# The end of a router on Trainium2: layer 1's modulation in steps between the slot table's groups, one-hot columns in pairs, a fixed TensorE order, and the last router tiles by twos

## The chip, the cores and the metric

The kernel runs on one core of one Trainium2 chip. The metric is the device time of the whole program in microseconds (us), and it is compared by the median of several runs. TensorE multiplies matrices into PSUM, VectorE (DVE), ScalarE (ACT) and GpSimd (POOL) work beside it, and SyncE (SP) issues most of the DMAs. The program is recorded by a tile framework: each engine has its own queue, which it runs in order, and a scheduler decides the order in the queues at build time, unless the source fixes it.

## The reference

Two transformer layers over 2048 tokens of width 512, in fp32. Each layer takes six modulation vectors from a matrix product of its own conditioning vector; they are needed for the normalisation (scale and shift) and for the gates of that layer's attention and feed-forward part.

```python
mod = (_silu(L1_c) @ L1_wmod).reshape(L1_c.shape[0], 6, 1, -1)
sa, ca, ga, sb, cb, gb = (mod[:, 0], mod[:, 1], mod[:, 2], mod[:, 3], mod[:, 4], mod[:, 5])
```

The feed-forward part of layer 0 is a mixture of 64 experts. A router picks eight experts for each token; experts that are only second choices may be mapped to similar first choices; every token then goes through its experts:

```python
logits = x @ gate_weight.T
probs = jax.nn.softmax(logits.astype(jnp.float32), axis=-1).astype(logits.dtype)
top_val, top_idx = lax.top_k(probs, TOP_K)
...
mapping = jnp.where(replace, best_primary, jnp.arange(E))
rerouted = mapping[top_idx]
...
gu = lax.ragged_dot(xs, jnp.swapaxes(gate_up_proj, 1, 2), group_sizes)
gate, up = jnp.split(gu, 2, axis=-1)
hact = jax.nn.silu(gate) * up
y = lax.ragged_dot(hact, jnp.swapaxes(down_proj, 1, 2), group_sizes)
...
out = jnp.zeros_like(x).at[tok].add(y * w[:, None])
```

Layer 1 has windowed attention and a dense feed-forward part; it needs the modulation of layer 1, and it comes after the experts.

## The kernel before

The kernel goes through layer 0's attention, the router, the experts in 32 pairs, layer 1's attention and layer 1's feed-forward part. The 2048 tokens are 16 tiles of 128. All matrix products go through one helper, `mm` at L129, so the profile names nearly all of them L129; they are told apart by the tiles that they write and read. An fp32 product shows as two instructions in the trace, an f16 product or a transpose as one.

**Router, first part.** It runs inside the attention's loop. After each fourth tile (`m % 4 == 3`), `route` (L417) puts two steps on a list, `logits` (L421) for the next turn of the loop and `choose` (L432) for the one after. `logits` normalises four tiles, transposes them (tiles nT_f, hTr), stores the normalised rows to `h_d` in DRAM, and multiplies by the gate (lg). `choose` takes the softmax and the eight largest values of each token, and leaves `sel` (f16 masks), its transpose `selT` (through st) and the normalised probabilities `pT` (through spT). The attention's own end for tile m is `project` (L383): transposes oT_a, a copy by ACT to oTs_a, and the product po_a, which DVE adds to `x_sb`.

**Router, second part** (from about L531). `cnt` counts the tokens of each expert and DVE copies it to c (L536). Then follow the mapping of experts, the running counts `pf` by token, and `perm`, the order of the experts by size (L599). `gps` gives the weights' row of each expert, and SP starts to load the first four experts' weights. `pw` (L614 to L622) carries the probabilities into the new order and to `h_d`; `ops_` (L637) gives the spill-over offsets that `shift` needs. From `pf` and `shift` DVE makes `vT` (L656 to L659): for each token and expert the slot that the token gets. `tv` transposes it, ACT copies it to `vm`, and `V.max` takes eight slots for each token.

**The slot table.** `tps` is a table in PSUM of 128 rows by 164 columns that ends up with the token of each slot. The 16 tiles go in four groups of four. For each tile DVE writes two one-hot tensors in f16, `hr` (128 rows by 8 choices, L677) and `hc` (164 columns by 8 choices, L680); ACT scales `hr` by the token's number (L678); and eight products add one choice each:

```python
for k in range(TOPK):
    mm(tps, hr[:, :, k], hc[:, :, k], n == 0, n == NT * TOPK - 1)
```

Both operands are read at a step of eight f16. `hr` and `hc` have three buffers each. DVE then turns the table into `tidx` (L687), and POOL gathers rows of `h_d` by it into `xring` (L507), 128 rows at a time and twelve places in all. Two small products, eps_ and rps, make lists for the loop that catches spill-over; DVE makes `of` (L697) between them.

**Modulation of layer 1.** `modulate(1, ...)` (L704) is recorded behind all this. For each of the six vectors a weight tile `wm` of 1 MB is loaded by SP (two buffers). Four vectors are needed as columns; each takes 16 products of 128 x 128 by a single column, 32 instructions in the trace. Two are needed as rows; each takes four products of 128 x 512. Where the scheduler puts these products among those of `tps` is its own choice.

**The first experts.** `turn(0)` transposes the gathered rows of experts 0 and 1 (xp, L734) and writes xT by DVE and ACT; `take(turn(0), 2 * KC)` does all eight of these steps before `gate_up` (L743) starts on the first pair. `shares(0)` copies the gathered probabilities (wc, L883). `fetch_w` and `fetch_x` fetch weights and rows two pairs ahead. `in_turn` (L714) is a scope in which the scheduler records an instruction behind the last TensorE instruction noted in `st_["pe"]`; it fixes an order in the queue and adds no wait on the chip.

Of the kernel before, what the change touches and what calls it, by code (L numbers as in the profile page):

```python
# [17 lines left out]
ALU = mybir.AluOpType  # L18
# [38 lines left out]
NX = 12  # L57

# [65 lines left out]
def block_kernel(ctx: ExitStack, tc: tile.TileContext, t: dict, out: bass.AP):  # L124
# [141 lines left out]
    with tc.tile_pool(name="a0", bufs=1) as ap, tc.tile_pool(name="a0k", bufs=1) as kp:  # L266
# [71 lines left out]
        with tc.tile_pool(name="rn", bufs=4) as rn, tc.tile_pool(name="a0s", bufs=2) as sp, tc.tile_pool(name="p_s", bufs=2, space=PSUM) as p_s, tc.tile_pool(  # L338
# [78 lines left out]
            def route(m, a):  # L417

                g = m - 3

                def logits():  # L421
                    hT = rn.tile([P, KC, D], F32, tag="hT", name=f"hTr_{g}", bufs=1)
                    normed_T(list(range(g, g + 4)), hT, 0, m0[4], m0[3], rn, p_m, "f0", "m", h_d)
                    lg = p_m.tile([P, 4, E], F32, tag="m", name=f"lg_{g}")
                    for b in range(4):
                        for c in range(KC):
                            mm(lg[:, b, :], hT[:, c, b * P : (b + 1) * P], gw[:, c, :], c == 0, c == KC - 1)
                    mx = small.tile([P, 4], F32, tag="lmx", name=f"lmx_{g}")
                    V.tensor_reduce(mx, lg, X, ALU.max)
                    V.tensor_tensor(pb[:, g : g + 4, :], lg, bc(mx, 2, E), ALU.subtract)  # L430

                def choose():  # L432
                    p4 = pb[:, g : g + 4, :]
                    S.activation(p4, p4, AF.Exp)
                    sm = small.tile([P, 4], F32, tag="lsm", name=f"lsm_{g}")
# [6 lines left out]
                    for b in range(4):  # L442
                        i = g + b
                        V.max(top[:, i, :], pb[:, i, :])
                        V.tensor_copy(t4[:, b, 0:4], top[:, i, 0:4])
                        V.match_replace(left[:, 0, b, :], t4[:, b, :], pb[:, i, :], -1.0)
                        V.match_replace(left[:, 1, b, :], top[:, i, :], pb[:, i, :], -1.0)
                    for c in range(2):
                        V.tensor_scalar(sel[:, g : g + 4, c, :], left[:, c], 0.0, None, ALU.is_lt)
                    st = p_m.tile([P, D], F32, tag="m", name=f"st_{g}")  # L450
                    for b in range(4):
                        mm(st[0:E, b * P : (b + 1) * P], sel[:, g + b, 1, :], ident16)
                    S.copy(selT[:, g * P : (g + 4) * P], st[0:E, :])

                    t4s = small.tile([P, 4], F32, tag="t4s", name=f"t4s_{g}")
                    V.tensor_reduce(t4s, top[:, g : g + 4, :], X, ALU.add)
                    V.tensor_scalar(t4s, t4s, 1e-12, None, ALU.max)
                    V.reciprocal(t4s, t4s)
                    V.tensor_tensor(p4, p4, sel[:, g : g + 4, 1, :], ALU.mult)
                    V.tensor_tensor(p4, p4, bc(t4s, 2, E), ALU.mult)  # L460
                    st = p_m.tile([P, 2, P], F32, tag="m", name=f"spT_{g}")
                    for b in range(2):
                        i = g + 2 * b
                        TE.transpose(st[:, b, :], pb[:, i : i + 2, :].rearrange("p i e -> p (i e)"), ident)
                    S.copy(pT[:, g // 2 : g // 2 + 2, :], st)
# [5 lines left out]
            for a in range(len(units) + 4):  # L471
                if a < len(units):
                    soft0(*units[a])
                if 0 < a <= len(units):
                    m, hf = units[a - 1]
                    value0(m, hf)
                    if hf == 1:
                        project(m, heads.pop(m), wo, sp, p_m, "a0")
                        if m % 4 == 3:
                            route(m, a)  # L480
# [24 lines left out]

    def gather(dst, src, idx):
# [18 lines left out]
    with tc.tile_pool(name="rw", bufs=1) as rw, tc.tile_pool(name="rh", bufs=3) as rh:  # L525
        with tc.tile_pool(name="p_q", bufs=3, space=PSUM) as p_q, tc.tile_pool(
            name="p_b", bufs=1, space=PSUM
        ) as p_b:
            id2, own = con("id2"), con("own")
# [71 lines left out]
            mm(gps, con("expert")[0:E, :], perm[0:E, :])  # L601
# [3 lines left out]

            mps = p_q.tile([E, P], F32, tag="q", name="mps")
            TE.transpose(mps, map2, ident)
            mapT = rw.tile([E, P], F32, tag="mapT", name="mapT")
            S.copy(mapT, mps)
            mps = p_q.tile([P, E], F32, tag="q", name="mrs")  # L610
            mm(mps, mapT, perm[0:E, :])
            mapr = rw.tile([P, E], F32, tag="mapr", name="mapr")
            S.copy(mapr, mps)
            pw = rw.tile([P, NT, E], F32, tag="pw", name="pw")  # L614
            pws = [p_q.tile([P, 8, E], F32, tag="q", name=f"pw_{b}") for b in range(2)]
            for a in range(NT // 2):
                for b in range(2):
                    r = slice(E * b, E * b + E)
                    mm(pws[b][:, a, :], pT[r, a, :], mapr[r, :])
            for b in range(2):  # L620
                S.copy(pw[:, b:NT:2, :], pws[b])
            nc.sync.dma_start(out=h_d[0:T, D:].rearrange("(i p) e -> p i e", p=P), in_=pw)  # L622
# [13 lines left out]
            V.tensor_copy(ot, ov_i)  # L636
            ops_ = p_q.tile([P, 2], F32, tag="q", name="ops_")  # L637
            mm(ops_[:, 0:1], con("upto")[0:E, :], ot[0:E, :])
            mm(ops_[:, 1:2], ones[0:E, :], ot[0:E, :])
# [6 lines left out]
            V.tensor_scalar(base1, base, 1.0, None, ALU.add)  # L646

# [4 lines left out]
            tps = p_b.tile([P, ST], F32, tag="tps", name="tps")  # L652
            n = 0
            for b in range(2):
                jump = rh.tile([P, D], F32, tag="jump", name=f"jump_{b}", bufs=2)
                V.tensor_scalar(jump, pf[:, b, :], room, shift, ALU.is_ge, ALU.mult)  # L656
                vT = rh.tile([P, D], F32, tag="vT", name=f"vT_{b}", bufs=2)
                V.scalar_tensor_tensor(vT, pf[:, b, :], base1, jump, ALU.add, ALU.add)
                V.scalar_tensor_tensor(vT, mT[:, b, :], 1.0, vT, ALU.min, ALU.mult)  # L659
                tv = p_q.tile([P, 4, 2, E], F32, tag="q", name=f"tv_{b}")  # L660
                for i in range(4):
                    TE.transpose(tv[:, i].rearrange("p h e -> p (h e)"), vT[:, i * P : (i + 1) * P], ident)
                for h in range(2):
                    i0 = 8 * h + 4 * b
                    i4 = slice(i0, i0 + 4)
                    S.copy(vm[:, i4, :], tv[:, :, h, :])
# [8 lines left out]
                    for i in range(i0, i0 + 4):  # L675
# [3 lines left out]
                        hc = rh.tile([P, ST, TOPK], F16, tag="hc", name=f"hc_{i}")  # L679
                        V.tensor_tensor(hc, iota8[:, 0:ST, :], bc(tlf[:, i, :], 1, ST), ALU.is_equal)  # L680
                        for k in range(TOPK):
                            mm(tps, hr[:, :, k], hc[:, :, k], n == 0, n == NT * TOPK - 1)
                            n += 1

# [19 lines left out]
            m1 = modulate(1, want, modp, rw, p_q, "q")  # L704
# [5 lines left out]
    with tc.tile_pool(name="h1", bufs=1) as h1, tc.tile_pool(name="p_x", bufs=2, space=PSUM) as p_x, tc.tile_pool(  # L710
        name="p_g", bufs=3, space=PSUM
    ) as p_g, tc.tile_pool(name="p_y", bufs=3, space=PSUM) as p_y:

        def in_turn():  # L714

            return tc.issue_after(st_["pe"].ins) if "pe" in st_ else nullcontext()
# [10 lines left out]
        def x_T(r, xs, n):  # L727
# [3 lines left out]
            def chunk(c):  # L731
# [6 lines left out]
                else:  # L738
                    V.tensor_scalar(xT[:, c, 0:n], xp[:, 0:n], sc, sh, ALU.mult, ALU.add)  # L739
# [3 lines left out]
        def gate_up(r, ws, xTs, n, between=None):  # L743

            hA = []
            for h, (w1, xT) in enumerate(zip(ws, xTs)):
                ps = []
# [145 lines left out]
        take(turn(0), 2 * KC)  # L893
        shares(0)
        for r in range(2, 4):
            fetch_x(r)
        for q in range(NQ):
# [3 lines left out]
            if q + 2 < NQ:  # L901
                for r in (2 * q + 4, 2 * q + 5):
                    fetch_w(r)
                    fetch_x(r)
            steps = turn(q + 1) if q + 1 < NQ else []
            with in_turn():
                hA, hB, last = gate_up(
                    q, [s["w"][0] for s in two], [s["xT"] for s in two], ROOM[q], lambda: take(steps, 2)
                )
            take(steps, 2)  # L910
# [334 lines left out]
def _layouts(a):  # L1245
# [10 lines left out]
    for n in (0, 1):  # L1256
        d[f"L{n}_c"] = cols(a[f"L{n}_c"].reshape(D))
        d[f"L{n}_wmod"] = a[f"L{n}_wmod"].reshape(KC, P, 6, D).transpose(2, 1, 0, 3)
# [48 lines left out]
```

## Time and profile before

| what | us |
|---|---|
| median of 3 runs (lowest, highest) | 2306.02 (2305.62, 2310.59) |
| the profiled execution | 2301.6 |
| its span, first to last instruction | 2299.8 |
| TensorE busy | 2122.3 (92%) |
| DVE, ACT, POOL busy | 847.7, 473.6, 559.0 |
| mean granted TensorE clock | 0.941 of full speed |
| last attention projection of layer 0 ends | 310.27 |
| first product of the slot table | 357.55 |
| slot table complete | 412.06 |
| first transpose of gathered rows | 435.94 |
| first product of expert 0 | 441.55 |

The page's section 2 cuts the span in 40 slices of 57.5 us and shows in tenths how busy each engine was and which share of the full clock TensorE was granted. The chain of waits follows the work that ended last back to the start: each row has its start, its length, its engine, the tile it writes, and its line. The windows give busy time by engine (instructions in brackets), the granted clock, the DMA engines' share and GB/s for a stretch of time. In the groups by shape, the number behind the bar is the total busy time in us and the mean of one instruction in ns; neighbours in a queue overlap, so that the distance from start to start can be shorter than the mean.

### The profile page before, as it was taken

Reading aid. Unit: us, or ns where it says so; the run is one execution under the profiler, and the core shown is the slowest. Engines: PE = TensorE matmul, PEld = TensorE weight load, DVE = VectorE, ACT = ScalarE, POOL = GpSimd, SP = SyncE. Lnnn points to the kernel's source line nnn. Section 1 sums busy time; section 2 is a strip of 40 time slices with the busy share of each in tenths; the row PEclk is TensorE's granted clock in tenths of the full one; section 3 lists DMA queues with packets and bytes.
Section 4 is the critical chain, followed back from the end, with each engine's and each line's share of the span. In section 5 each row is a group of like instructions: output and inputs, shape, how many; then the busy total and the mean of one; then the engine's idle time right before and its main releaser. Section 6 shows DMA issues by size and latency. Waiting matters only on the chain.

```text
span 2299.8 us, 27707 instructions
## 1 busy us (share of the span) xinstructions
PE 2122.3 (92%) x10584; PEld 1178.8 (51%) x10584; DVE 847.7 (37%) x2177; ACT 473.6 (21%) x1114; POOL 559.0 (24%) x444
## 2 busy tenths in 40 slices
PE   3999978999999999999639999997999999999999
PEld 3665645545555566676315555554444444444444
DVE  3246655154544433345366456554011011000101
ACT  0124413111111111111001356653010010010000
POOL 2300000365665666654424100000010010010000
PEclk9899975799999999999869899998999999999999
DMA  9800113589899899999752000005000000000000
GB/s 355 299 2 19 38 58 110 166 200 224 220 236 235 208 244 239 253 301 313 163 195 59 19 2 1 2 2 218 2 0 19 0 0 4 15 0 0 19 0 19
DMA packets 137350, 256.40 MB, mean 111 GB/s; under 512 B 52649, under 2 KB 55657, under 8 KB 134657
## 3 DMA queue, kind: packets, MB, share of 16 engines
q1 hardware_dynamic: 95136, 159.48, 20.9%
q0 software_dynamic: 36032, 77.30, 16.2%
q10 hardware_dynamic: 6048, 17.83, 2.1%
q8 instruction: 85, 1.39, 0.2%
q14 instruction: 49, 0.39, 0.1%
HBM read 180.56 MB, written 71.65 MB: 110 GB/s over the span
## 4 chain that ended last, share of the span: by engine, by line
PE 81%; DVE 6%; DMA 6%; ACT 4%; issue 1%; POOL 1%; ACTq 0%; POOLq 0%; SPq 0%; DVEq 0%
PE y L129 18%; PE gu L129 10%; PE up L129 9%; PE gate L129 9%; PE gub L129 5%; PE xp L734 3%; PE q L129 3%; ACT pr L1106 3%; PE s L129 3%; PE po L129 2%; PE mod L129 2%; PE po_a L129 2%; DMA sum<-yo,tidx 2%; PE o L129 2%; PE pt L1124 2%; PE tps L129 2%
## 5 line engine op out<-in xcount | busy, mean ns | idle before, releaser
L793 POOL DMA_INDIRECT sum<-yo,tidx x164 | 268.7, 1638 | 120.6 <-DMA sum<-yo,tidx 36.5
L507 POOL DMA_INDIRECT xring<-h_d,tidx x164 | 168.0, 1025 | 510.9 <-DVE tidx L687 331.3
L1231 DVE SCALAR_TENSOR_TENSOR act<-up,L_ws_up,sg 128x512 f32<-128x512 f32 x64 | 48.1, 751 | 598.6 <-PE up L129 598.6
L129 PE MATMUL gu<-xT,w 128*128 128x312 f32 (+26 forms) x1024 | 245.5, 398 | 6.6 <-DVE xT L739 6.6
L129 PE MATMUL gate<-xh,wug 128*128 128x512 f32 x512 | 230.7, 592 | 0.0
L129 PE MATMUL up<-xh,wug 128*128 128x512 f32 x512 | 230.7, 592 | 0.0
L129 PE MATMUL y<-wd,act 128*128 128x512 f32 x512 | 229.5, 592 | 0.0
L129 PEld LDWEIGHTS gu<-xT,w 128*128 128x128 f32 x1024 | 191.7, 192 | 60.7 <-issue 16.5
L1229 ACT ACTIVATE sg<-gate,L_ws_gate 128x512 f32<-128x512 f32 x64 | 44.0, 687 | 575.4 <-PE gate L129 575.4
L129 PEld LDWEIGHTS up<-xh,wug 128*128 128x128 f32 x512 | 97.3, 190 | 122.5 <-issue 122.5
L129 PEld LDWEIGHTS y<-wd,act 128*128 128x128 f32 x512 | 97.3, 190 | 122.5 <-issue 122.5
L129 PEld LDWEIGHTS gate<-xh,wug 128*128 128x128 f32 x512 | 96.8, 190 | 119.6 <-issue 119.6
L129 PE MATMUL y<-w,hA 128*128 128x512 f32 (+22 forms) x328 | 148.8, 596 | 0.9 <-DVE yo L789 0.9
L789 DVE SCALAR_TENSOR_TENSOR yo<-y,wc,modr 128x512 f32<-128x512 f32 (+22 forms) x164 | 117.1, 745 | 80.1 <-PE y L129 68.4
L737 ACT ACTIVATE xT<-xp,modc,modc 128x312 f32<-128x312 f32 (+26 forms) x128 | 74.3, 580 | 316.0 <-PE xp L734 286.3
L1200 POOL TENSOR_TENSOR xh<-hT 128x1024 f32<-128x1024 f32 x3 | 7.6, 2524 | 503.3 <-DVE xn_f L229 335.9
L1106 ACT ACTIVATE pr<-ng,nb 128x208 f32<-128x208 f32 (+1 forms) x256 | 115.4, 453 | 55.1 <-DVE nb L1096 55.1
L129 PE MATMUL gub<-xT,w 128*64 128x312 f32 (+26 forms) x1024 | 125.4, 398 | 0.0
L734 PEld LDWEIGHTS xp<-cst,xring 128*128 128x128 f32 x656 | 72.3, 141 | 68.1 <-issue 46.6
L734 PE MATMUL xp<-cst,xring 128*128 128x128 f32 x656 | 98.3, 282 | 1.9 <-DVE xT L739 1.2
L755 DVE TENSOR_TENSOR hA<-hA,gu 128x312 f32<-128x312 f32 (+26 forms) x64 | 28.2, 440 | 186.7 <-PE xp L734 99.6
L129 PEld LDWEIGHTS gub<-xT,w 128*64 128x64 f32 x1024 | 70.5, 137 | 44.8 <-issue 11.3
(311 smaller groups left out, 2662.6 us busy)
## 6 DMA issues: line engine op xcount, KB each, us to landing
w<-in_L_gu SPq DMA_DIRECT2D x64, 768.0 KB, 7.3
sum<-xring SPq DMA_DIRECT2D x5, 4352.0 KB, 21.9
w<-in_L_dn SPq DMA_DIRECT2D x64, 256.0 KB, 8.3
wm<-in_L_wmod SPq DMA_DIRECT2D x9, 1024.0 KB, 6.8
w<-in_L_dn SPq DMA_DIRECT2D x64, 128.0 KB, 8.7
sa<-sum SPq DMA_DIRECT2D x32, 256.0 KB, 9.0
h_d<-xn_f SPq DMA_DIRECT2D x16, 256.0 KB, 2.9
wda<-in_L_Wdown SPq DMA_DIRECT2D x8, 512.0 KB, 13.9
```

Source lines behind the costliest of these rows:

```text
L129: return TE.matmul(o, lhsT, rhs, start=start, stop=stop)
L507: return G.indirect_dma_start(out=dst, out_offset=None, in_=src[:, :], in_offset=bass.IndirectOffsetOnAxis(ap=idx, axis=0))
L734: st_["pe"] = TE.transpose(xp[:, b * P : (b + 1) * P], xg[:, c * P : (c + 1) * P], ident)
L737: S.activation(xT[:, c, 0:n], xp[:, 0:n], AF.Identity, bias=sh, scale=sc)
L755: V.tensor_tensor(o[:, 0:n], o[:, 0:n], ps[1][:, 0:n], ALU.mult)
L789: V.scalar_tensor_tensor(yo, ys[h], shares[h][rows, b : b + 1], m0[5][rows, :], ALU.mult, ALU.mult)
L793: G.indirect_dma_start(out=sums[k][:, :], out_offset=bass.IndirectOffsetOnAxis(ap=idx, axis=0), in_=yo, in_offset=None, compute_op=ALU.add,)
L1106: S.activation(prs[i, j][:, c, :nk], ng[:, :nk], AF.Exp, bias=nb, scale=-1.0, accum_out=totals[i][:, c, j : j + 1],)
L1124: TE.transpose(pt[0:n, c, :], pr[:, c, b * P : b * P + n], ident)
L1200: eng.tensor_tensor(b[:, :, 0, :], a[:, :, 0, :], a[:, :, 1, :], ALU.add)
L1229: S.activation(sg, pg, AF.Silu, scale=wsg[:, f : f + 1])
L1231: V.scalar_tensor_tensor(acts[f], pu, wsu[:, f : f + 1], sg, ALU.mult, ALU.mult)
```

## The change

- `route(g, n, a)` takes a number of tiles. The router runs after tiles 4, 8 and 12 with four tiles, and after 14 and 16 with two.
- `in_turn` moves up, and `next_mm` and `next_T` record a product or a transpose behind the last noted one. From `gps` on, the TensorE order is the order in which the source names the instructions. `ops_` stands in front of `pw`, and both `vT` are made before `tv`.
- `hc` becomes four blocks of 164 columns by two choices. `iota8` is read two choices wide, and a product reads `hc` at a step of two f16.
- Layer 1's modulation no longer goes vector by vector but in four steps over the contraction: step k takes one 128-row slice of all six vectors. The weights' layout in DRAM is changed to match. The four column vectors are made as rows on four column groups of the array (32 rows of the result each), then turned by four transposes; the two gates are made with 128 rows. A step stands behind each of the first three groups of the table and one behind the table. `wm` now has one buffer, `wg` two; the load of step k+1 is recorded behind step k.
- The rows of expert 1 are transposed between the two halves of the first `gate_up`, and weights and rows of the third pair are fetched behind it. The wc copies stand behind the last xT that DVE wrote.
- In TensorE's queue, `rps` now stands behind the second group of the table; it stood behind the third.

```diff
+ROUTED = {4: 4, 8: 4, 12: 4, 14: 2, 16: 2}
...
-                        if m % 4 == 3:
-                            route(m, a)
+                        if m + 1 in ROUTED:
+                            n = ROUTED[m + 1]
+                            route(m + 1 - n, n, a)
...
+    def in_turn():
+
+        return tc.issue_after(st_["pe"].ins) if "pe" in st_ else nullcontext()
+
+    def next_mm(*a):
+        with in_turn():
+            st_["pe"] = mm(*a)
...
+            def mod_load(k):
+                w = rw.tile([P, 4, D], F32, tag="wm", name=f"wm_1_{k}")
+                nc.sync.dma_start(out=w, in_=t["L1_wmod"][k, :, 0:4, :])
+                wg = rw.tile([P, 2, D], F32, tag="wg", name=f"wg_1_{k}", bufs=2)
+                nc.sync.dma_start(out=wg, in_=t["L1_wmod"][k, :, 4:6, :])
+                mod_w[k] = w, wg
+
+            mod_load(0)
...
-            mm(gps, con("expert")[0:E, :], perm[0:E, :])
+            next_mm(gps, con("expert")[0:E, :], perm[0:E, :])
...
-            mm(ops_[:, 0:1], con("upto")[0:E, :], ot[0:E, :])
-            mm(ops_[:, 1:2], ones[0:E, :], ot[0:E, :])
+            next_mm(ops_[:, 0:1], con("upto")[0:E, :], ot[0:E, :])
+            next_mm(ops_[:, 1:2], ones[0:E, :], ot[0:E, :])
...
+            mods = [p_b.tile([P, 2, D], F32, tag=g, name=f"mod_{g}") for g in ("mT", "pf")]
+            cs1 = csil[:, 1, :]
+            csb = rw.tile([P, KC, P], F32, tag="csb", name="csb_1")
+            S.copy(csb, bc(cs1, 2, P))
+
+            def mod_step(k):
+                w, wg = mod_w.pop(k)
+                for u in range(4):
+                    next_mm(mods[0][32 * u : 32 * u + 32, 0, :], csb[:, k, 0:32], w[:, u, :], k == 0, k == KC - 1)
+                for u in range(2):
+                    next_mm(mods[1][:, u, :], csb[:, k, :], wg[:, u, :], k == 0, k == KC - 1)
+                if k + 1 < KC:
+                    mod_load(k + 1)
...
-                        hc = rh.tile([P, ST, TOPK], F16, tag="hc", name=f"hc_{i}")
-                        V.tensor_tensor(hc, iota8[:, 0:ST, :], bc(tlf[:, i, :], 1, ST), ALU.is_equal)
+
+                        hc = rh.tile([P, 4, ST, 2], F16, tag="hc", name=f"hc_{i}")
+                        two = tlf[:, i, :].rearrange("p (a c) -> p a c", c=2)
+                        V.tensor_tensor(hc, bc(iota8[:, 0:ST, 0:2], 1, 4), bc(two, 2, ST), ALU.is_equal)
                         for k in range(TOPK):
-                            mm(tps, hr[:, :, k], hc[:, :, k], n == 0, n == NT * TOPK - 1)
+                            next_mm(tps, hr[:, :, k], hc[:, k // 2, :, k % 2], n == 0, n == NT * TOPK - 1)
                             n += 1
+                    if 2 * b + h < 3:
+                        mod_step(2 * b + h)
...
-            m1 = modulate(1, want, modp, rw, p_q, "q")
+            mod_step(3)
+            m1 = {}
+            mrow = rw.tile([P, D], F32, tag="mrow", name="mrow")
+            S.copy(mrow, mods[0][:, 0, :])
+            for u, n in enumerate((2, 5)):
+                m1[n] = modp.tile([P, D], F32, tag=f"mod1{n}", name=f"modr_1_{n}")
+                S.copy(m1[n], mods[1][:, u, :])
+            mcol = mods[0][:, 1, :].rearrange("p (c q) -> p c q", c=KC)
+            for c in range(KC):
+                next_T(mcol[:, c, :], mrow[:, c * P : (c + 1) * P], ident)
...
-        take(turn(0), 2 * KC)
-        shares(0)
+        opening = turn(0)
+        take(opening, KC)
+        with tc.issue_after(st_["xv"].ins):
+            shares(0)
...
                 hA, hB, last = gate_up(
-                    q, [s["w"][0] for s in two], [s["xT"] for s in two], ROOM[q], lambda: take(steps, 2)
+                    q, [s["w"][0] for s in two], [s["xT"] for s in two], ROOM[q], lambda: take(steps, 2),
+                    lambda: take(opening, KC),
                 )
+            if q == 0:
+                fetch(2)
```

## The prediction

> **What bounds the kernel now.** I read the page first (sections 1 and 2), then the chain of waits between 295 and 455 us, where nearly all of the edits lie, then the windows, the groups by shape and the timelines of each engine there.
>
> ```profile
> PE 2122.3 (92%) x10584; PEld 1178.8 (51%) x10584; DVE 847.7 (37%) x2177; ACT 473.6 (21%) x1114; POOL 559.0 (24%) x444
> PEclk9899975799999999999869899998999999999999
> ```
>
> TensorE is the bound nearly everywhere, and its granted clock sags in slices 6 to 8 (287 to 460 us): that is the end of the router. The chain there (start, length):
>
> ```profile
> 347.25 0.76 PE ops__2719 L129 x4
> ...
> 357.55 28.65 PE tps L129 x96
> 386.20 0.93 PE rps L129 x2
> 387.13 13.74 PE mod L129 x64
> 400.87 7.14 PE tps L129 x24
> 408.01 1.71 PE mod L129 x2
> 409.73 2.34 PE tps L129 x8
> 412.06 8.62 PE mod L129 x38
> ...
> 420.70 9.03 DMA wm<-in_L_wmod
> ...
> 429.86 5.41 PE mod L129 x8
> ```
>
> Two things stand out. The 128 matmuls of the slot table take 298 ns each (28.65/96), and layer 1's modulation sits half between them (15.4 us) and half behind them: expert 0's first transposes come only at 435.94 us, 23.9 us after the table. Clock, and what the form of an operand costs:
>
> ```profile
> 312.00:315.00 3.00, 1.79 (x8) 0.98 (x8) 2.10 (x6) 0.26 (x1) 0.00 (x0) 0.81 0.37 134
> 357.00:387.00 30.00, 29.45 (x98) 14.38 (x98) 21.61 (x53) 15.24 (x14) 0.00 (x0) 0.50 0.14 38
> 414.00:417.00 3.00, 3.00 (x9) 1.31 (x7) 0.00 (x0) 0.17 (x1) 2.39 (x3) 0.62 1.03 251
> L680 DVE TENSOR_TENSOR hc<-iota,tlf 128x1312 f16<-128x1312 f16 x16 | 13.4, 834 | 0.0
> L129 PE MATMUL tps<-hc,hr 128*128 128x164 f16 x128 | 38.5, 477 | 2.3 <-ACT hr L678 2.3
> 336.25 0.31 PE L129 MATMUL pf<-ones,acc 128*64 128x128 f16 x1
> 336.36 0.31 PE L129 MATMUL pf<-ltri,selm 128*64 128x128 f16 x1
> 1372.86 1.08 PE L129 MATMUL o<-pts,v 80*32 80x256 f32 x8
> 417.77 0.92 POOL L507 DMA_INDIRECT xring<-h_d,tidx  x1 [0.30 <-issue]
> ```
>
> The column before the DMA share is the granted clock. The pf matmuls, whose moving operand is contiguous, follow each other every 107 ns for 128 columns at the same half clock: 0.83 ns a column. tps takes 1.82 ns a column, with hc read at a step of 8 f16 (16 bytes). The reading is what is slow, not the array.
>
> **The change part by part** (minus is time saved on the path)
>
> *A. The last four tiles of the router by twos.* The path runs from the end of tile 13's output projection po_a (298.69) to the count copy c (331.52): 32.8 us. Afterwards TensorE's fixed order is: lg of 12 and 13, only then oT and po of tile 14, st of 12/13, spT, oT and po of tile 15, then lg of 14 and 15. So the first pair's chain is put in front of the last two projections, and ACT loads Sqrt and Exp tables twice (1.28 us each, from the timeline of ACT). Rows: x_sb add 0.7, bn 0.7, xn 0.56 each, halved hTr about 0.55, lg 1.76 at full clock (32 took 3.52) or 3.55 at half (7.10), choose for two tiles about 3.2 (5.2 for four, 324.98 to 330.2). Laid out: lg of 12/13 ends at 306.9, po of 14 at 311.7, st at 312.4, pb's last multiply at 314.3 (behind a 0.7 add and a 0.7 bn on DVE), oT and po of 15 until 319.4, its add, statistics, xn, transposes until 324.9, lg until 326.6, choose until 329.8, c at 330.8: -0.7. That is with the full clock. In the trace the clock fell to half in the windows that follow one 2.9 us gap of TensorE. Here there are gaps of 2 to 3 us before po of 15 and after it. po takes 3.7 at full, at most 6.8 at half; two of them, transposes and lg all at half give +9. I take +3: po of 15 partly at half (+1.5), the last lg at half (+1.8), transposes (+0.5), less the 0.7.
>
> [...] the window says 0.50 for more than 50 us. The measurement decides: a matmul that waits on its operand does not warm the clock here, while six dense 512-column fp32 matmuls did (0.62, then 0.95 after 417).
>
> *B. ops_ in front of pw.* ot is ready at 343.1, but ops_ stood behind 3.68 us of pw in TensorE's queue and ran at 347.25. Ahead of it, it ends at 344.1; more_f, shift and the two vT follow (348.03 to 351.75 before), so vT of b=0 is ready at 347.8. pw (until 347.8) hides under that DVE work; tv starts at 347.9 in place of 351.88: -3.9. The pw store on SP waits for ACT until 349, earlier than before.
>
> *C. hc as four blocks of pairs.* The bytes are the same, 1312 f16 on DVE, 0.76 us start to start (0.83 mean). But iota8 is now read in pairs at a 16-byte step. No DVE row of the trace does this. [...] By the row alone (0.76) the table would end about 3 us earlier than I sum below. The trace's nearest row is TensorE's own 16-byte step (1.82 ns an element)[...]. I take 1.3, ends 0.76 and 1.75. On the path once at the start: +0.5.
>
> *D. The table.* On TensorE, hc is then read at 4 bytes. By pf's 0.83 ns a column, 164 columns are 137 ns; the weights hr keep their step of 16 bytes, and their load is 145 ns (PEld rows of hr, 142/145/309). I take 145 ns, so a tile of eight is 1.16 us in place of 2.39. DVE needs hr 0.61 + hc 1.3 + 0.23 (tidy-up per tile) = 2.14 us a tile, ACT 1.16: DVE becomes the limit while only tiles run. Between the groups stand three steps of modulation: 4 products of 32 rows on four column groups and 2 of 128. The o row: 8 of 256 columns on column groups, the next such row 0.85 us later (1373.71), half the serial price (po_a: 0.45 for 512). So the four cost 1.7 and the two 1.7 at full clock, 6.8 in all at half; [...] I take 4.7 (between 3.4 and 6.8). hr and hc have three buffers, so DVE runs three tiles ahead during a step. From the first tile: group 1 ends at 5.7, step 0 at 10.4, group 2 at 15.0. Then comes a wait that was not there: rps now stands behind group 2 in TensorE's queue and needs "of", which DVE makes only after hr and hc of the third tile of group 3, and that hr needs group 2's buffers. Hence of at 20.2; TensorE idles 5 us with step 1 and group 3 queued behind. rps to 21.1, step 1 to 25.8, group 3 to 30.5, step 2 to 35.2, group 4 to 39.9. Before: 412.06 - 357.55 = 54.5. So -14.6; -18 with hc at 0.76, -8 with hc at 1.75 and slow steps.
>
> Loads: wm has one buffer now; the next 1 MB leaves SP's queue when four products are done, and lands 5 to 9 us later (6.8 median on the page, 12.2 at most). Steps are 15, 10 and 9 us apart from there, so they just fit.
>
> *E. Behind the table.* Before: 23.9 us to the first xp, 29.5 to the first gu (441.55). After: hole and tidx 0.8, POOL starts at +1.7, its fourth gather at +5.7 (413.76 to 417.77), landing 2.8 to 5.9 us later (the tile view of xring: 2.8 least, 5.9 median). So xp of expert 0 has its rows at +10.3. Meanwhile step 3, mrow 0.6 and four transposes 1.1 end at about +7, hidden under the gathers with 3 us to spare; the ACT copies of the two gates as well. gu of expert 0 begins at +12.7. The other expert's xp (2.9 us, half of the 5.6 that both took) now stands between the two gu[...]. gu of both ended at 453.4, 41.3 after the table; now 12.7 + 5.9 + 1.7 + 2.9 + 5.9 = 29.1: -12 (ends -14 and -8). The wc copies moved behind xT wait for the eighth gather, at +17, with hA at +19 behind them: free. Weights and gathers of experts 4 and 5 are ordered behind gate_up(0), but POOL's order is the same as before and w1 waits for those buffers anyway: nothing, and q=2 needs them 60 us later.
>
> **Sum.** +3 - 3.9 + 0.5 - 14.6 - 12 = -27.0. The profiled execution took 2301.6 us (span 2299.8), so 2274.6; the median of the runs shown is 4.4 above that, 2306.0, and against it I predict 2279.
>
> **The rivals**
>
> 1. The pairs do not shorten tps: the weights' 16-byte step, untouched, sets the 298 ns. For it: PEld of hr and the matmul alternate. Against it: its load takes 145 of the 298. The table would be 38.2 + three steps of 4.7 to 6.8 + 3.4 of rps and its wait, about 58.5: +4 in place of -14.6, in all -8.4, 2298.
>
> 2. The half clock at the end of the router (+9) together with modulation loads that arrive at the 12.2 us maximum (+5.5 before step 2, +2.5 in the tail): -27 + 6 + 8 = -13, 2293. For it: the 0.50 from 315 on. Against it: the wm loads meet fewer gathers than before.
>
> 3. Slower than before, by one mechanism: DVE does not keep its packed rate in L680's new form, with runs of only two elements[...] It decides from about 3.1 us per hc; below that the other gains carry it. [...]
>
> **How the numbers follow.** A measurement of this kernel tells about 0.2% (4.6 us) from no change. Forecast 0.71, rival 1 0.12, rival 2 0.12, rival 3 0.05. Faster: 0.71 + 0.12 + most of rival 1 (0.09) = 0.92; same 0.03; slower 0.05. Best ends together (-0.7, -3.9, 0, -18, -14) are -36.6: 2269; the forecast's worst (+9, -3.9, +1, -8, -8) is about -10. The range 2267 to 2297 holds the forecast, rival 2 and half of rival 1.
>
> **What would show it.** Right: tps starts every 140 to 150 ns within a tile, hc at 1.2 to 1.7 us, an idle TensorE of some 5 us before rps, table under 43 us, the first xp 9 to 12 us after tidx, gu directly behind. A is right if c comes 0 to 6 us later in that part, with the half clock already before po of tile 15. Wrong: tps at 298 ns; hc above 3 us; step 1 or 2 waiting for wm; or a first xp that waits for step 3 and not for its rows.

## The result, and the profile after

| | before | changed kernel |
|---|---|---|
| median, us (lowest, highest; runs) | 2305.82 (2301.39, 2310.59; 4) | 2281.01 (2278.45, 2284.87; 4) |
| ratio, 95% interval | | 0.9893 [0.9869, 0.9918] |
| profiled execution, its span, us | 2301.6, 2299.8 | 2280.16, 2278.2 |
| slot table, first tps to last | 54.5 (357.55 to 412.06) | 36.3 (354.07 to 390.39) |
| last tps to first gub of expert 0 | 41.9 | 34.9 |
| first gub to the end of the span | 1845.9 | 1852.9 |

gu and gub are the products of `gate_up`: gu the first 128 columns of gate and of up, one expert after the other, gub the last 64 columns of both experts.

The change is worth 24.8 us by the medians; 27 were predicted (2306 to 2279). Two further sets of the changed kernel (y1_same and z1_same below) gave ratios of 0.9903 [0.9880, 0.9926] and 0.9882 [0.9860, 0.9905]; the median of all twelve of its runs is 2281.9.

The page after, TensorE's busy time and its granted clock in 40 slices. The sag of slices 6 to 8 is now 0.8 and 0.7 in slices 6 and 7:

```profile
PE 2081.9 (91%) x10492; PEld 1149.6 (50%) x10492; DVE 856.8 (38%) x2193; ACT 477.9 (21%) x1123; POOL 558.6 (25%) x444
PEclk9899987999999999999779899998999999999999
```

TensorE's timeline around the table (start, length, what it did, and in brackets its idle time before and what ended it):

```profile
354.07 2.41 PE L131 MATMUL tps<-hc,hr 128*128 128x164 f16 x16 [2.73 <-ACT hr L725]
...
359.20 1.06 PE L131 MATMUL mod_mT<-wm,csb 128*32 128x512 f32 x8
360.20 1.98 PE L131 MATMUL mod_pf<-wg,csb 128*128 128x512 f32 x4
...
366.80 0.79 PE L131 MATMUL tps<-hc,hr 128*128 128x164 f16 x8 [1.05 <-DVE hc L729]
373.90 0.97 PE L131 MATMUL rps<-of,ones 64*128 64x191 f32 x2 [6.31 <-DVE t8b L717]
374.80 1.94 PE L131 MATMUL mod_mT<-wm,csb 128*32 128x512 f32 x8
376.66 2.73 PE L131 MATMUL mod_pf<-wg,csb 128*128 128x512 f32 x4
379.23 2.02 PE L131 MATMUL tps<-hc,hr 128*128 128x164 f16 x24
```

Eight tps take 0.8 us where they took 2.4, and nearly every tile now waits for DVE's hc or ACT's hr. The new wait stands before rps: 6.31 us. A step takes 3 us at full clock and 4.6 when it starts at half. The windows (us, busy time with instructions of PE, PEld, DVE, ACT, POOL, then granted clock, DMA share, GB/s) show TensorE empty while DVE is full, and after that the full clock:

```profile
354.00:357.00 3.00, 2.77 (x19) 2.52 (x20) 3.00 (x4) 2.21 (x3) 0.00 (x0) 0.50 1.07 317
370.00:373.00 3.00, 0.00 (x0) 0.00 (x0) 3.00 (x4) 2.81 (x3) 0.00 (x0) 0.50 0.00 0
384.00:390.00 6.00, 4.25 (x34) 3.04 (x35) 5.54 (x6) 3.45 (x3) 0.00 (x0) 1.00 0.53 175
```

The groups by shape: hc has become dearer, and tps, in time on the array, 38.5 to 13.5 us.

```profile
L729 DVE TENSOR_TENSOR hc<-iota,tlf 128x1312 f16<-128x1312 f16 x16 | 21.5, 1342 | 0.0
L131 PE MATMUL tps<-hc,hr 128*128 128x164 f16 x128 | 13.5, 259 | 8.3 <-DVE hc L729 5.1 <-ACT hr L725 3.2
```

Behind the table, TensorE's timeline shows the transposes of expert 0's rows starting as the rows land, then expert 0's gu, and a wait inside the transposes of expert 1:

```profile
397.11 0.41 PE L796 MATMUL xp<-cst,xring 128*128 128x128 f32 x2 [3.37 <-DMA xring<-h_d,tidx]
...
399.30 1.12 PE L796 MATMUL xp<-cst,xring 128*128 128x128 f32 x4 [0.97 <-DMA xring<-h_d,tidx]
...
402.80 7.42 PE L131 MATMUL gu<-xT,w 128*128 128x440 f32 x16
...
416.25 1.97 PE L796 MATMUL xp<-cst,xring 128*128 128x128 f32 x8 [5.16 <-DVE xT L801]
```

The chain of waits has a row there whose cause the profile does not name:

```profile
404.67 10.28 another core or an unknown queue x2
414.95 0.60 DVE hA L819
415.55 0.66 DVE xT L801
416.25 1.97 PE xp L796 x8
418.22 6.44 PE gu L131 x16
```

So at the first gub the kernel is 28.7 us ahead of the one before (425.25 against 453.95), and at the end of the span 21.6.

### The profile page after: what moved, and what is told of

Read it like the earlier page. It is cut to its first block, busy times and chain, and to the rows that moved or that the text cites. A ratio compares the mean times of both kernels' runs of the same rounds, so it can differ in the third digit from the quotient of the medians.

```text
span 2278.2 us, 27545 instructions
## 1 busy us (share of the span) xinstructions
PE 2081.9 (91%) x10492; PEld 1149.6 (50%) x10492; DVE 856.8 (38%) x2193; ACT 477.9 (21%) x1123; POOL 558.6 (25%) x444
## 4 chain that ended last, share of the span: by engine, by line
PE 78%; DVE 7%; DMA 6%; ACT 4%; issue 2%; POOL 1%; another core or an unknown queue 0%; ACTq 0%; POOLq 0%; SPq 0%; DVEq 0%
PE y L131 18%; PE gu L131 10%; PE up L131 9%; PE gate L131 9%; PE gub L131 5%; PE xp L796 3%; PE q L131 3%; ACT pr L1179 3%; DMA sum<-yo,tidx 3%; PE s L131 3%; PE po L131 2%; PE o L131 2%; PE po_a L131 2%; PE pt L1197 2%; PE v L131 1%
## 5 line engine op out<-in xcount | busy, mean ns | idle before, releaser
L857 POOL DMA_INDIRECT sum<-yo,tidx x164 | 269.2, 1642 | 119.5 <-issue 37.5
L796 PE MATMUL xp<-cst,xring 128*128 128x128 f32 x656 | 101.0, 286 | 10.5 <-DVE xT L801 5.2
```

Of the source, the lines that this page charges most:

```text
L796: st_["pe"] = TE.transpose(xp[:, b * P : (b + 1) * P], xg[:, c * P : (c + 1) * P], ident)
L857: G.indirect_dma_start(out=sums[k][:, :], out_offset=bass.IndirectOffsetOnAxis(ap=idx, axis=0), in_=yo, in_offset=None, compute_op=ALU.add,)
```

## The experiments

Three questions: what of the table's gain comes from which part; whether the last tiles by twos and the split of the first experts' rows help; and what the row of 10.28 us is. All but the runs on the kernel before start from the changed kernel. "After the table" below is the time from the last tps.

**x1_rps_late.** The wait before rps is taken away.

```diff
-            mm(rps, ones[0:E, :], of)
-            V.tensor_copy(rank_more, rps)
-
             mod_step(3)
+            next_mm(rps, ones[0:E, :], of)
+            V.tensor_copy(rank_more, rps)
```

> The changed kernel, with rps (and rank_more) moved in TensorE's queue from behind the table's second group to behind the last modulation step. Theory: the 6.3 us in which TensorE idles before rps hold up step 1 and the third group, and DVE then stands 4.9 us for a buffer of hr; without the wait the table is as long as DVE's own work, 16 tiles of about 2.1 us: 36.3 us becomes 31 to 32, the whole program 4 to 5 us shorter (2276). Rival: the weights of step 1 have only just landed by then, so TensorE waits for wm in place of rps, and the table stays at 35 us or more.

Measured: 2270.88 (2268.76 to 2272.09), ratio 0.9834 [0.9818, 0.9851]; table 30.8 us. TensorE's timeline at the place of the old wait:

```profile
372.37 0.78 PE L131 MATMUL tps<-hc,hr 128*128 128x164 f16 x8 [1.06 <-DVE hc L729]
373.07 1.06 PE L131 MATMUL mod_mT<-wm,csb 128*32 128x512 f32 x8
374.07 1.98 PE L131 MATMUL mod_pf<-wg,csb 128*128 128x512 f32 x4
376.56 0.84 PE L131 MATMUL tps<-hc,hr 128*128 128x164 f16 x8 [0.51 <-ACT hr L725]
```

Step 1 follows at once; wm was there, so the rival falls. The wait cost the table 5.5 us. The total fell by more than the 4 to 5 us expected, by 11 us against the twelve runs of the changed kernel: gub, too, begins 4.3 us earlier after the table (+30.6 for +34.9), which is taken up with the late semaphores below. No run of the changed kernel is on record from the chip of x1 to x4, so how much of these 4.3 us is the edit's and how much the chip's is not shown.

**x2_contig.** hc's comparison reads adjacent pairs.

```diff
+    iota2 = rp.tile([P, ST, 2], F16, tag="iota2", name="iota2")
...
+            V.tensor_copy(iota2, bc(iota[:, 0:ST], 2, 2))
...
-                        V.tensor_tensor(hc, bc(iota8[:, 0:ST, 0:2], 1, 4), bc(two, 2, ST), ALU.is_equal)
+                        V.tensor_tensor(hc, bc(iota2, 1, 4), bc(two, 2, ST), ALU.is_equal)
```

> The changed kernel, with the pairs that hc is compared to read from a tile of their own in which the pairs are adjacent (164 x 2 f16), in place of iota8 at a step of 16 bytes. Theory: hc went from 0.76 to 1.28 us only because of that step; adjacent pairs bring it back to about 0.76, a tile costs DVE 1.6 us, the table takes about 28 us in place of 36.3, and the program is 8 us shorter (2273) unless the modulation's loads become late. Rival: runs of two elements are what costs DVE (the other operand also changes every two), then hc stays at 1.2 to 1.3 us and the time at 2281.

Measured: 2268.7 (2263.37 to 2275.26), 0.9838 [0.9821, 0.9854]; table 31.5 us. The group by shape:

```profile
L731 DVE TENSOR_TENSOR hc<-iota,tlf 128x1312 f16<-128x1312 f16 x16 | 13.3, 833 | 0.0
```

1342 ns are 833 again, the 834 of the kernel before: the 16-byte step was the whole surcharge, and runs of two elements cost DVE nothing. The table fell by 4.8 us and not by the 8 expected: the wait before rps stayed (4.42 us here) and step 1 behind it ran at half clock (5.4 us).

**x3_before_pairs.** Only the pairs, in the kernel before (the three lines of hc and the product's index from the diff above).

> The kernel before, with hc in four blocks of pairs and nothing else changed. Theory: tps drops from 298 to 150 ns or less each, DVE becomes the limit of the table at 2.1 us a tile, and the table, with the 15.4 us of modulation still in it, takes 43 to 47 us in place of 54.5; program 2306 becomes 2296 to 2298. Rival 1 of the prediction (the weights' step of 16 bytes sets the 298 ns): tps stays at 298 ns and the table at 54 us or more, 2306.

Measured: 2292.13 (2287.62 to 2294.47), 0.9933 [0.9916, 0.9950]; table 40.1 us. The group by shape:

```profile
L129 PE MATMUL tps<-hc,hr 128*128 128x164 f16 x128 | 17.8, 316 | 11.0 <-ACT hr L678 8.7 <-DVE hc L681 1.9
```

The pairs alone take 14.4 us off the table, more than the 7.5 to 11.5 expected, and 15.0 off the first gub (438.93); the time, too, is below the 2296 to 2298 expected. Rival 1 of the prediction falls here. The 12.4 us of modulation inside the table do not cost their full length: behind them the 24 tps of three tiles follow at once, in 3.29 us (392.43), which DVE had made ready meanwhile.

**x4_combo.** x1 and x2 together.

> The changed kernel with both edits: adjacent pairs for hc, and rps behind the last modulation step. Theory: DVE needs about 1.6 us a tile, 25 us in all, and the four steps 3 us each; the table takes 24 to 28 us in place of 36.3, limited by the loads of wm (one buffer, a step at most every 7 us or so): 2269 to 2272. Rival: the loads take 9 to 12 us each, the steps wait, the table stays above 31 us and the gain is no larger than that of one edit alone.

Measured: 2265.58 (2263.86 to 2274.36), 0.9812 [0.9796, 0.9828]; table 27.1 us, 9.3 less than the changed kernel's. A new wait of 1.80 us for wm before step 1 keeps it from the full 5.5 + 4.8.

**y4_eight.** hc back in its old form, all other parts kept.

```diff
-                        hc = rh.tile([P, 4, ST, 2], F16, tag="hc", name=f"hc_{i}")
-                        two = tlf[:, i, :].rearrange("p (a c) -> p a c", c=2)
-                        V.tensor_tensor(hc, bc(iota8[:, 0:ST, 0:2], 1, 4), bc(two, 2, ST), ALU.is_equal)
+                        hc = rh.tile([P, ST, TOPK], F16, tag="hc", name=f"hc_{i}")
+                        V.tensor_tensor(hc, iota8[:, 0:ST, :], bc(tlf[:, i, :], 1, ST), ALU.is_equal)
...
-                            next_mm(tps, hr[:, :, k], hc[:, k // 2, :, k % 2], n == 0, n == NT * TOPK - 1)
+                            next_mm(tps, hr[:, :, k], hc[:, :, k], n == 0, n == NT * TOPK - 1)
```

> The changed kernel, with hc in its old form (164 x 8, read by TensorE at a step of 16 bytes), the steps of modulation and all else left in. Theory: tps takes 298 ns again and sets the table's length: 38 us of tps and three steps of 3 to 5 us, 48 to 54 us in place of 36.3; DVE's hc falls to 0.83 us but is no longer the limit; the program 13 to 17 us longer, 2293 to 2298. Rival: the steps warm the clock, and at full clock the 16-byte step costs half; then tps takes 150 to 200 ns behind each step, and the table stays under 42 us.

Measured: 2300.92 (2292.0 to 2306.16, 20 runs), 0.9972 [0.9961, 0.9982]; table 55.8 us, both a little above what was expected. Windows of the tps instructions alone (PE, DVE, clock, DMA share, GB/s):

```profile
372.00:384.00 12.00, 5.60 (x19) 0.00 (x0) 0.50 0.05 9
385.00:391.00 6.00, 5.58 (x19) 0.00 (x0) 1.00 0.55 203
```

Nineteen tps take 5.6 us at half clock and at full clock. From start to start the median is 297 ns at 0.5 and 296 ns at 1.0. So the 16-byte step is a limit that the clock does not move, and the rival, half the time at full clock, falls. With adjacent pairs the same product takes 136 ns at half and 77 ns at full clock.

**y2_fours.** The router's last four tiles in one group again.

```diff
-ROUTED = {4: 4, 8: 4, 12: 4, 14: 2, 16: 2}
+ROUTED = {4: 4, 8: 4, 12: 4, 16: 4}
```

> The changed kernel, with the last four router tiles in one group of four as before. Theory: the twos gain nothing, since they add idle gaps of TensorE and with them the half clock: from the end of po_a of tile 13 to c it takes 32.8 us as in the kernel before, against 33.8 in the changed kernel and 37.5 in one of its variants; the program is 1 to 4 us shorter than the changed kernel, 2277 to 2280. Rival: the twos do hide the first pair's chain under the last two projections, and without them c comes later than 34 us after po_a of tile 13.

Measured: 2278.77 (2276.44 to 2280.39), 0.9871 [0.9855, 0.9888], beside y1_same with 2283.53 on the same chip. From the end of po_a of tile 13 to c: 32.76 us, as in the kernel before (32.75). With the twos it is 33.5 us in five profiles (the first, x2, y3, y4, z2) and 37.5 to 38.3 in four (y1, z1, x1, x4). The windows show where it is lost; first the first profile of the changed kernel, then x1_rps_late, with the same instructions:

```profile
302.00:305.00 3.00, 2.03 (x13) 1.32 (x13) 1.46 (x3) 1.13 (x2) 0.00 (x0) 1.00 0.48 178
305.00:312.00 7.00, 6.11 (x30) 3.36 (x28) 3.29 (x21) 2.34 (x4) 0.00 (x0) 1.00 0.00 0
```

```profile
302.00:305.00 3.00, 1.60 (x16) 0.95 (x14) 2.32 (x6) 1.22 (x3) 0.00 (x0) 1.00 0.18 69
305.00:312.00 7.00, 6.04 (x25) 5.22 (x26) 1.14 (x4) 1.85 (x4) 0.00 (x0) 0.52 0.13 47
```

In x1 the clock went to half before lg of tiles 12 and 13: lg took 3.68 us for 2.00, po_a of tile 14 5.68 for 3.70. Everything ran 1.7 us later there, so the stretches of 3.41 us in which the trace's clock records go (last section) cut the same gaps around the transposes elsewhere: the stretch behind po_a of tile 13 held 57% of matmul time in x1 and 65% in the first profile (49 to 57% in the four slow profiles, 61 to 68% in the five others). That this share decides is likely and not shown, as the first profile kept its full clock behind a later stretch of 55%. The group of two never pays: it costs 0.8 us at best, and 4.7 to 5.5 in four of nine profiles.

**y3_tail_old.** The rows of experts 0 and 1 both ahead of the first gate_up.

```diff
-        take(opening, KC)
+        take(opening, 2 * KC)
         with tc.issue_after(st_["xv"].ins):
```

> The changed kernel, with the rows of experts 0 and 1 both transposed before the first gate_up, as before. Theory: the split hides little, since expert 1's rows have landed 14 us after the table anyway and the first gu then ran cold: gu begins at +16 to +17 in place of +12 to +14, gub at +29 to +31.5 in place of about +31, the time within 1.5 us of the changed kernel's. Rival: the split hides the 2.9 us of xp of expert 1, as the prediction's step E has it; then gub begins at +33 to +34 and the program is 3 us longer.

Measured: 2279.61 (2278.15 to 2285.64), 0.9886 [0.9866, 0.9907]; gu begins at +19.9, gub at +33.5 after the table. gu began 3 us later than expected. The gub is where the rival put it, but the rival reckoned from +31, and the control on the same chip, y1_same with the split, has +34.9. The times decide nothing: y1_same has 2283.53, but its profile has the slow form of the router's end (37.5 us) and this one the fast form (33.5). Among executions with late semaphores (below) the split shows no gain; without them this kernel was not seen, so what it hides there stays open.

**y1_same, z1_same, z2_split, w1_before.** These four are about the row of 10.28 us. (A semaphore update is the profile's record of one engine telling another that a result is ready.) DVE's timeline there, in the first profile of the changed kernel and in x1_rps_late:

```profile
404.52 0.15 DVE L947 COPY wc<-xring 56x1 f32<-56x1 f32 x1 [0.38 <-DMA xring<-h_d,tidx]
414.94 0.61 DVE L819 TENSOR_TENSOR hA<-hA,gu 128x440 f32<-128x440 f32 x1 [10.27 <-remote]
```

```profile
404.32 0.68 DVE L946 COPY wc<-xring 128x1 f32<-128x1 f32 x8
412.13 0.61 DVE L818 TENSOR_TENSOR hA<-hA,gu 128x440 f32<-128x440 f32 x1 [7.14 <-PE xp L795]
```

In the first, hA waits for a gu whose record ends at 410.22, but the update of TensorE's semaphore is recorded at 414.85, 4.6 us later, and five more, of products that end from 410.3 to 411.1, follow within 0.2 us. In x1, where no update is late, gub begins at +30.6.

> The changed kernel once more, nothing edited. In its first profile DVE stood still from 404.7 to 414.9 us and ACT nearly as long, though the products that they waited for were recorded as done at 407.3 and 410.2; that execution also lost an eighth of its semaphore records. Theory: this belongs to that one execution, and not to the order of the instructions; then gub of expert 0 begins about 31 us after the table (as in the three variants run so far), not 34.9. Rival: sixteen gathers back to back hold the semaphores of TensorE up; then the stop is there again and gub begins at +34 to +35.

Measured: 2283.53 (2280.92 to 2290.27); gub at +34.87, updates up to 4.9 us late again (ACT's hA starts at 417.35 on a gu that ended at 412.42). My theory of a single disturbed execution fell.

> The changed kernel a third time, nothing edited, as the control for the two runs beside it. Up to now DVE and ACT stood still until 24.5 us after the table in the five profiles of the changed kernel, y2_fours and y4_eight (and less in y3_tail_old), all of which lost semaphore records, and never in the four profiles x1 to x4, which lost none and came from another chip. Theory (the chip, or its recording, is what differs): the stop is in all three runs of this set or in none. Rival (the order of the instructions causes it): it is in this run, gub at +34 to +35, and not in z3_best, whose rps and hc are those of x4_combo.

> The changed kernel, with the gathers of experts 2 and 3 made to wait for the first xT of expert 1 (one copy of a column on POOL stands ahead of them), so that POOL issues eight gathers in a row and not sixteen. Theory: the stop ended in every case just as the sixteenth gather landed; with eight in a row it ends, if it is there at all, before +15, and gub begins at about +31. Rival: the gathers have no part in it; if z1_same shows the stop, this run shows it too, at +34 or later.

z2_split puts this in front of the gathers of experts 2 and 3 and records these in the first gate_up:

```diff
...
+                    G.tensor_copy(gate, st_[1]["xT"][:, 0, 0:1])
+                    for r in range(2, 4):
+                        fetch_x(r)
...
```

Measured: z1_same 2281.82 (2276.36 to 2285.07), gub at +34.87, updates up to 6.5 us late (ACT's hA starts at 419.45 on a gu that ended at 412.96); z2_split 2281.18 (2278.55 to 2283.49), gub at +33.5, updates up to 4.5 us late. The edit of z2 missed its aim: in POOL's timeline the scheduler has put the copy behind the sixteenth gather, so sixteen still went in a row, and the run says nothing about their number. z3_best, in the same set, has late updates too (1.9 to 2.5 us; gub at +32.9), which x4_combo, with the same rps and hc, has not (+31.4).

> The kernel before, nothing edited, for one more profile. TensorE's semaphores came late behind the table in all seven profiles that lost an eighth of their semaphore records (chips 0 and 7 where the chip is known), z3_best among them, and in none of the four of chip 3, which lost none. If this profile loses records too, theory (the chip or its recording): late semaphores are seen here as well, somewhere behind the table, and gub begins later than the 41.9 us after the table of the first profile; rival (the changed order): none are late and gub begins at +41 to +42. If it loses no records, both expect +41 to +42 and it tells nothing of this.

Measured: 2309.2 (one run); this profile lost records as well, one update is 1.5 us late (429.83, a product of the modulation), and gub begins at +43.7 in place of +41.9.

So late updates of over half a microsecond behind the table (in the 45 us there) are in all nine profiles that lost about an eighth of their semaphore records (14500 to 14800 are left, against 16900 to 17000), the kernel before among them, and in none of the five that lost none (the first of the kernel before, and x1 to x4, which came from one chip). The changed order alone is not the cause, as the kernel before has one too. It may pay more: 3.5 to 4.3 us in the changed kernel (+34.9 against +30.6 to +31.4 in x1, x2 and x4, which are edited kernels), against 1.8 in the kernel before. The sixteen gathers may have a part: in seven of the nine profiles the last burst begins within 0.5 us of the end of their packets (414.85 and 414.52 in the first). But x1, x2 and x4 issue the same sixteen in a row and show no late update, and z2, which was to test this, did not. Whether the chip or its recording delays the updates, and whether the gathers help, stays open.

**z3_best.** x4_combo with the group of four (ROUTED as in y2_fours).

> The changed kernel with three edits: adjacent pairs for hc, rps behind the last modulation step, and the last four router tiles in one group of four. Theory: table 27 us as in x4_combo, and from po_a of tile 13 to c 32.8 us in place of 38.3; so 2 to 5 us below x4_combo, 2261 to 2264, if the stop behind the table is not there, 2266 to 2268 if it is. Rival: the four-tile group cools the clock before the table and gives the difference back: no shorter than x4_combo, 2265 to 2270.

Measured: 2267.54 (2264.7 to 2268.47, 5 runs), 0.9818 [0.9802, 0.9833]; on the same chip the changed kernel had 2281.82. Table 25.3 us, po_a of tile 13 to c 32.75. TensorE's timeline:

```profile
361.31 2.05 PE L131 MATMUL tps<-hc,hr 128*128 128x164 f16 x24
364.13 0.85 PE L131 MATMUL tps<-hc,hr 128*128 128x164 f16 x8 [0.77 <-DVE s L717]
365.56 1.06 PE L131 MATMUL mod_mT<-wm,csb 128*32 128x512 f32 x8 [0.57 <-DMA wm<-in_L_wmod]
366.55 1.98 PE L131 MATMUL mod_pf<-wg,csb 128*128 128x512 f32 x4
```

The table is now as long as DVE's work (16 x 1.6 us); only 0.57 us is a wait for wm. It beats both kernels: 14 us below the changed one. Against x4_combo nothing is shown: the medians are 2 us apart, on different chips, and z3 carries late updates.

## Why the prediction was right, and where its terms were off

The table's part, the largest, came by the mechanism that was predicted: x3 and y4 show the step of hc as its cause. That the sum came so close is in part luck: the table gained 3.6 us more than its term, the part behind it lost 5 us, and the router's end falls on either side of its +3.

| step | predicted | measured | by |
|---|---|---|---|
| A, router's end | +3 (-0.7 to +9) | +0.8 or +4.7 to +5.5; mean of nine profiles +2.6 | po_a of tile 13 to c |
| B, ops_ before pw | -3.9 | -4.4 from c to tv | 20.44 to 16.01 |
| C, hc before the first tps | +0.5 | +0.5 from tv to tps | 5.67 to 6.13 |
| D, table | -14.6 | -18.2 | 54.5 to 36.3 |
| E, behind the table | -12 | -7.0; -10.5 to -11.3 without late updates (x1, x2, x4) | last tps to gub, 41.9 to 34.9 |
| sum at the first gub | -27.0 | -28.7, and -23.4 in y1_same and z1_same | 453.95 to 425.25, 430.6 |

**A** was right on the average, which is luck, as its form was wrong. I expected the half clock before po_a of tile 15 as a part of every execution. It comes either before lg of tiles 12 and 13 or, as in the first profile, only at lg of 14 and 15.

**B and C** came as worked out; tv began at 347.94, as predicted. hc takes 1.22 to 1.28 us from start to start, where 1.3 was taken, with 1.75 as the upper end; both were my estimates, as no DVE row of the trace had such a read. x2 confirms the step as its cause: with adjacent pairs hc takes 833 ns for 1342, so DVE keeps the rate of before (834) in runs of two. By the row of before alone hc would have cost 0.76.

**D** was too small by 3.6 us, through two terms. Nearly all of it fell behind rps, where the third group took 3.6 us and step 2 2.8, each put at 4.7. A tps was put at 145 ns, by the load of its weights; it takes 136 ns at half and 77 ns at full clock, so the weights were no limit. And a step was put at 4.7 us, my estimate between the full and the half clock: four products of 32 rows on four column groups cost what one costs (the eight instructions of mod_mT took 1.06 us; eight of 128 rows would take 4, by the 1.98 us of mod_pf's four), not half of the serial price, which I had drawn from the o row; why that row shows only half stays open. At full clock a step is 3.0 us. The wait before rps was there as predicted, 6.3 us for 5, and x1 shows its price. x3 and y4 together show whose gain it is: the pairs alone bring -14.4, all else without the pairs +1.3, both -18.2, so the rest pays only together with the pairs.

**E** hit the start of gu, +12.4 for +12.7, and step 3 was hidden, but the way there was another. The first xp did not wait for all four gathers (+10.3): it began at +6.7 with the first rows, 5.9 us after tidx and not 9 to 12, and the last of expert 0's rows were there by +9.2. The transposes then took longer than the 2.4 us put down for them, from +9.2 to +12.4, so the two errors cancelled. The 1.7 us in E's sum was my estimate for a start of gu at half clock; the granted clock was 0.50 until 405.5, and gu of expert 0 took 7.42 us, 1.5 more than half of the 11.82 that the gu of both took in the kernel before, at full clock. Behind gu most of the missing 5 us lies in the wait of 5.16 us before 416.25: TensorE waits there for an xT that DVE wrote only after the late update of 414.85. In x1, x2 and x4, without late updates, E is -10.5 to -11.3. The split had no share in the 12: the prediction's own sum kept the 2.9 us of expert 1's transposes in full, and y3 shows no gain from it.

**The remainder.** 28.7 us ahead at gub became 21.6 at the end. The work is the same, but the span after gub varies from 1845.9 to 1854.6 us over fourteen profiles, and it goes with the granted clock (133 us of it at half clock in the shortest, 155 in the longest). In the windows from the last y of the experts to the first gate product, the kernel before, then the changed one, then x4_combo:

```profile
1132.30:1601.40 469.10, 385.99 (x3077) 225.57 (x3078) 263.32 (x819) 193.94 (x638) 71.91 (x88) 0.88 0.19 57
```

```profile
1103.80:1578.40 474.60, 391.07 (x3077) 227.67 (x3077) 263.29 (x819) 194.02 (x638) 71.04 (x88) 0.87 0.18 54
```

```profile
1096.60:1573.00 476.40, 391.65 (x3077) 226.42 (x3077) 262.93 (x819) 194.37 (x638) 73.33 (x89) 0.86 0.19 55
```

The instructions agree, the clock goes from 0.88 to 0.86, and the time with it, 469 to 476 us. The first profile of the kernel before is the shortest of the fourteen there; another, w1_before, has 1852.4 from gub to the end. So no price of the change is shown in this part, only the scatter of the runs, and the difference of two single profiles would have said 21.6 where the medians say 24.8.

## What to carry to other kernels

Ask of a slow matmul whether its time changes with the granted clock: if it doesn't (here 297 ns at half and 296 at full clock), suspect the way its operand is read. Here a layout with smaller steps was worth 14.4 us by itself although it made the writer dearer, and the reordering without it made the table 1.3 us longer. Then give the writer what it needs too: with adjacent pairs on both sides the same edit cost DVE nothing (833 ns for 834). When a fixed order takes the place of a scheduler's, look for products that wait on an engine running ahead of them (rps): one misplaced 1 us product cost the table 5.5 us. And a rearrangement that opens small gaps in TensorE's work must gain more than the clock can take: here the gain was below zero, -0.8 us at best and -4.7 to -5.5 in four of nine profiles.

## What the hardware showed that I had not expected

- A product with its moving operand at a 16-byte step took 297 ns for 164 columns at half clock and 296 ns at full clock; adjacent pairs, 136 and 77 ns.
- In the trace's clock records every stretch within a run is a multiple of 3.41 us. Over all fourteen profiles, by the matmul records in stretches of that length, the clock never stayed full behind one in which TensorE was busy less than 41%, and it fell behind about a third of those of 41% to 80%. It never rose behind one busy less than 82%. In the first profiles of the two kernels alone, it fell behind 17 of 17 under 41% and behind 15 of 52 of 41% to 80%, and the least busy one behind which it rose held 85%. The same instructions, shifted by 1.7 us, gave 33.5 or 37.5 us.
- Products that follow each other without a gap need not hold the clock: in y4_eight it fell from 1.00 to 0.50 at 391.5 in a row of 32 such products of 297 ns, though in the kernel with pairs it rose to 1.00 at 357.7 under nothing but tps.
- TensorE's semaphore updates reached DVE and ACT up to 6.5 us late (z1_same), mostly in bursts, in the nine executions whose profile lost records. What held them up, no run here shows.
